# A four-layer image network on one core: the frequency gate cut into links, with the pyramid of means on GpSimd

## The chip, the cores and the metric

The kernel runs on one core of a Trainium2 chip. The core has a matmul engine (TensorE, PE in the profile; its weight loads are PEld), three engines for other arithmetic (VectorE or DVE, ScalarE or ACT, GpSimd or POOL) and a queue engine that issues transfers (SyncE or SP). Every engine works through its own list of instructions in order and waits on semaphores for the others. The metric is the device time of one execution in microseconds (us); less is better.

## The reference

The input is a batch of four images of 192 channels and 64 x 64 pixels in fp32. Four layers follow each other: L0 (channel attention, a deformable convolution with a gather, an MLP), L1 (non-local attention), L2 (attention in overlapping windows, a projection, a frequency gate, a gated MLP) and L3 (a depthwise convolution with generated weights). The change touches the frequency gate of L2 alone:

```python
def _hft(x, w, b):
    a = 3.0 * x
    for s in (2, 4, 8):
        pool = x.reshape(B, C, h // s, s, ww // s, s).mean(axis=(3, 5))
        a = a - jnp.repeat(jnp.repeat(pool, s, axis=2), s, axis=3)
    return jax.nn.sigmoid(_dwconv3(a, w, b)) * x
...
out = _hft(_conv1x1(out, proj_w, proj_b), hft_w, hft_b)
x1 = x + out
```

From three times the projected image the means over blocks of 2 x 2, 4 x 4 and 8 x 8 pixels are subtracted; a 3 x 3 depthwise convolution and a sigmoid make a gate of that, and the gate multiplies the projected image.

## The kernel before

The 192 channels lie on 96 partitions in two halves. An image of 4096 pixels is worked on in `NCH` = 8 chunks of `CN` = 512 pixels, which are 8 rows of 64. The four images go through L2's second part one after the other in `rest`, which runs three generators in a row: `project` (projection and frequency gate), `mlp` and `layer3`. For images 0, 1 and 2 the MLP of layer 0 of the next image (`mlp0`) is interleaved with them: each `yield` of the three gives a credit of 0.5 or 1, and for each full credit one part of `mlp0` is issued. Image 3 has no next image; `rest` calls it `alone`. There five of the nine taps of the convolution go to TensorE (`HFT_PE`), as matmuls with diagonal weights (L1169) that GpSimd builds when the stage starts (L264); for images 0 to 2 all nine taps are VectorE's.

In `project` the order of the instructions on each engine is the order in which the code issues them, moved by a scheduler within what buffers and priorities allow, so that pieces of the gate stand between one another and between pieces of `mlp0`.

`first(i)` makes chunk i. Four matmul calls make the projection in PSUM (`pp`, L1197; the trace shows an fp32 matmul call as two records). ScalarE adds the bias and writes `pr` (L1200), of which there are three buffers. VectorE then builds the pyramid of means in 13 instructions: at each of three levels it adds the even and the odd rows into `pt` (L1208: 512, 128 and 32 elements per partition in the three levels) and the even and the odd columns into `pq` (L1211: 256, 64 and 16). Three multiplications by 1/4, 1/16 and 1/64 follow (L1214: 256, 64 and 16), and four additions of a coarser level into the next finer one (L1219: two of 32, two of 128). ScalarE writes three times `pr` into a strip `hft` of ten rows (L1224), of which `strips` holds three in turn, and VectorE subtracts the upsampled means from it in four instructions (L1230). `share(i)` lets GpSimd copy two edge rows between strip i and strip i-1 (L1151 and L1152); before that `get(i)` has GpSimd clear the side columns (L1140, L1141).

`second(i)` works on a chunk whose strip and whose neighbour's first row are there: nine taps for each half of the channels (the first L1175, the others L1177, into `ha`; the last three taps read the row that L1151 copied), the sigmoid on ScalarE (L1237), the product with `pr` (L1239) and the addition to the image `x` (L1240). It runs one chunk behind:

```python
for i in range(NCH):
    first(i)
    yield 0.5
    if i > 0:
        second(i - 1)
        yield 1.0
ahead()
second(NCH - 1)
```

`ahead()` issues the layer norm of the first chunk of `mlp`.

Of the kernel before, what the change touches and what calls it, by code (L numbers as in the profile page):

```python
# [10 lines left out]
F32 = mybir.dt.float32  # L11
I32 = mybir.dt.int32
AF = mybir.ActivationFunctionType
ALU = mybir.AluOpType
# [4 lines left out]
B, C, H, W = 4, 192, 64, 64  # L19
HW = H * W  # L20
P = 96
NCH = 8
CN = HW // NCH
# [46 lines left out]
def conv_seq_kernel(ctx: ExitStack, tc: tile.TileContext, a, out: bass.AP):  # L70
    nc = tc.nc

    def pool_of(**kw):

        return tc.tile_pool(**({} if kw.get("space") == DRAM else {"reuse_waits": "tile"}), **kw)
# [25 lines left out]
    def halves(name, pool=None):  # L101
        return halves_of(name, a[name].rearrange("(k p) n -> p k n", p=P), pool or wpool)
# [156 lines left out]
    def diagonals(name, w, m, taps, pool):  # L259
        p = w.shape[0]  # L260
        t = pool.tile([p, m, len(taps), p], F32, tag=f"diag_{name}", name=f"diag_{name}")
        for k in range(m):
            for j, tap in enumerate(taps):
                nc.gpsimd.tensor_scalar_mul(t[:, k, j, :], ident[:p, :p], w[:, k, tap : tap + 1])  # L264
        return t
# [3 lines left out]
    with pool_of(name="zero", bufs=1) as zp:  # L269
        zero = zp.tile([128, 4 * C], F32, tag="zero", name="zero")  # L270
        nc.gpsimd.memset(zero, 0.0)
        for i in range(2):
            t = dram.tile([TROWS, 4 * C], F32, tag=f"table{i}", name=f"table{i}")
            first, last = 2 * WP + 2, WP + 1 + NT * 128
# [857 lines left out]
    def strips(held):  # L1132


        tiles = {}

        def get(i):
            if i not in tiles:
                t = tiles[i] = held[:, i % held.shape[1]]
                nc.gpsimd.memset(t[:, :, :, 0:1], 0.0)  # L1140
                nc.gpsimd.memset(t[:, :, :, W + 1 : W + 2], 0.0)  # L1141
                if i == 0:
                    nc.gpsimd.memset(t[:, :, 0, 1 : W + 1], 0.0)
                if i == NCH - 1:
                    nc.gpsimd.memset(t[:, :, 9, 1 : W + 1], 0.0)
            return tiles[i]

        def share(i):

            if i > 0:  # L1150
                nc.gpsimd.tensor_copy(get(i - 1)[:, :, 9, 1 : W + 1], get(i)[:, :, 1, 1 : W + 1])  # L1151
                nc.gpsimd.tensor_copy(get(i)[:, :, 0, 1 : W + 1], get(i - 1)[:, :, 8, 1 : W + 1])  # L1152

        return get, share

    def depthwise(strip, w, k, diag, taps, acc, ps, name):


        parts = strip.shape[0]

        def src(tap):
            return strip[:, k, tap // 3 : tap // 3 + 8, tap % 3 : tap % 3 + W]

        to = acc.rearrange("p (r c) -> p r c", c=W)
        last = None
        if taps:
            p = ps.tile([128, CN], F32, tag="t", name=name)[:parts]
            for j, tap in enumerate(taps):
                nc.tensor.matmul(p, lhsT=diag[:, k, j, :], rhs=src(tap), start=j == 0, stop=j == len(taps) - 1)  # L1169
            last = p.rearrange("p (r c) -> p r c", c=W)  # L1170
        for tap in range(9):
            if tap in taps:
                continue
            if last is None:
                nc.vector.tensor_scalar_mul(to, src(tap), w[:, k, tap : tap + 1])  # L1175
            else:
                nc.vector.scalar_tensor_tensor(to, src(tap), w[:, k, tap : tap + 1], last, ALU.mult, ALU.add)  # L1177
            last = to

    def project(b, x, oi, ps, taps, ahead):  # L1180


        with ExitStack() as s:
            sb = s.enter_context(pool_of(name="l2b", bufs=2))
            s1 = s.enter_context(pool_of(name="l2b1", bufs=1))
            projT = halves("projT", s1)
            hft_diag = diagonals("hft", V["l2_hftw"], 2, taps, s1) if taps else None
            get, share = strips(s1.tile([P, 3, 2, 10, W + 2], F32, tag="hft", name=f"hft_{b}"))
            prs = {}

            def first(i):
                pr = sb.tile([P, 2, CN], F32, tag="pr", name=f"pr_{b}_{i}", bufs=3)
                prs[i] = pr
                for h in range(2):
                    p = ps.tile([128, CN], F32, tag="h", name=f"pp_{b}_{i}_{h}")[:P]
                    for k in range(2):
                        nc.tensor.matmul(  # L1197
                            p, lhsT=projT[:, k, bass.ts(h, P)], rhs=oi[:, k, bass.ts(i, CN)], start=k == 0, stop=k == 1
                        )
                    nc.scalar.activation(pr[:, h, :], p, AF.Identity, bias=V["l2_projb"][:, h])  # L1200

                sums = [pr.rearrange("p k n -> p (k n)").rearrange("p (r c) -> p r c", c=W)]
                for lev in range(3):
                    src = sums[-1]
                    nr, ncol = src.shape[1], src.shape[2]
                    pairs = src.rearrange("p (r e) c -> p e r c", e=2)
                    t = sb.tile([P, nr // 2, ncol], F32, tag=f"pt{lev}", name=f"pt_{b}_{i}_{lev}")
                    nc.vector.tensor_tensor(t, pairs[:, 0], pairs[:, 1], ALU.add)  # L1208
                    pairs = t.rearrange("p r (c e) -> p e r c", e=2)
                    q = sb.tile([P, nr // 2, ncol // 2], F32, tag=f"pq{lev}", name=f"pq_{b}_{i}_{lev}")  # L1210
                    nc.vector.tensor_tensor(q, pairs[:, 0], pairs[:, 1], ALU.add)  # L1211
                    sums.append(q)
                for lev in range(1, 4):
                    nc.vector.tensor_scalar_mul(sums[lev], sums[lev], 0.25**lev)  # L1214
                for lev in (2, 1):
                    fine = sums[lev].rearrange("p (r e) (c f) -> p e r c f", e=2, f=2)
                    coarse = sums[lev + 1]
                    for e in range(2):
                        nc.vector.tensor_tensor(  # L1219
                            fine[:, e], fine[:, e], coarse.unsqueeze(3).to_broadcast(list(coarse.shape) + [2]), ALU.add  # L1220
                        )
                t = get(i)
                for k in range(2):
                    nc.scalar.activation(  # L1224
                        t[:, k, 1:9, 1 : W + 1], pr[:, k, :].rearrange("p (r c) -> p r c", c=W), AF.Copy, scale=3.0
                    )
                    for e in range(2):
                        to = t[:, k, 1 + e : 9 : 2, 1 : W + 1].rearrange("p r (c f) -> p r c f", f=2)
                        mean = sums[1][:, 4 * k : 4 * k + 4, :]
                        nc.vector.tensor_tensor(to, to, mean.unsqueeze(3).to_broadcast([P, 4, 32, 2]), ALU.subtract)  # L1230
                share(i)

            def second(i):
                acc = sb.tile([P, 2, CN], F32, tag="acc", name=f"ha_{b}_{i}")
                for k in range(2):
                    depthwise(get(i), V["l2_hftw"], k, hft_diag, taps, acc[:, k, :], ps, f"ht_{b}_{i}_{k}")
                    nc.scalar.activation(acc[:, k, :], acc[:, k, :], AF.Sigmoid, bias=V["l2_hftb"][:, k])  # L1237
                cols = bass.ts(i, CN)
                nc.vector.tensor_tensor(acc, acc, prs.pop(i), ALU.mult)  # L1239
                nc.vector.tensor_tensor(x[:, :, cols], x[:, :, cols], acc, ALU.add)  # L1240

            for i in range(NCH):
                first(i)
                yield 0.5
                if i > 0:
                    second(i - 1)
                    yield 1.0
            ahead()
            second(NCH - 1)
            yield 1.0  # L1250

    def mlp(b, x, sums, sb, ps, taps, hn):

# [266 lines left out]
    second = begun.enter_context(pool_of(name="l0second", bufs=1))  # L1520
    with ExitStack() as s:
        sb = s.enter_context(pool_of(name="l0first", bufs=1))
# [14 lines left out]
    with ExitStack() as s:  # L1537
        sb, pool = (s.enter_context(pool_of(name=n, bufs=1)) for n in ("norms0", "l0d0"))
# [4 lines left out]
    for b in range(B):  # L1543
        with ExitStack() as s:
            sb = s.enter_context(pool_of(name="l1x", bufs=1))
# [22 lines left out]
        sums = stats.tile([P, 2, NCH], F32, tag="sums", name=f"sums_{b}")  # L1568
# [86 lines left out]
```

## Time and profile before

| what | value |
|---|---|
| median of 3 runs | 7346.84 us (7320.97 to 7362.43) |
| the profiled execution | 7341.43 us, span 7339.6 us, granted TensorE clock 0.924 |
| PE busy | 6582.3 us (90% of the span) |
| DVE busy | 5103.1 us (70%) |
| ACT busy | 3759.7 us (51%) |
| POOL busy | 2130.0 us (29%), of which the issue of gathers at L523 1674.8 us |

The profile is a page on one execution, the trace holds its single instructions, and the views named below are tables made of that trace. A duration is the time of one instruction on its engine, waits for other engines left out. On VectorE a new instruction starts about 0.08 us before the record of the one ahead of it ends, so what an instruction takes of the queue is read from the distance between two starts. "Idle before" and "releaser" tell how long an engine stood still ahead of an instruction and who ended that. The stage of `project` stands at about 1992 to 2160 us for image 0, 3692 to 3862 us for image 1, 5420 to 5589 us for image 2 and 6880 to 6993 us for image 3.

### The profile page before, as it was taken

The numbers are of one execution on the slowest core, as the hardware profiler recorded it, in microseconds if no ns is written. First come the engines' busy times: TensorE is split into PE (matmuls) and PEld (weight loads), VectorE is DVE, ScalarE is ACT, GpSimd is POOL, SyncE is SP. The second block draws the span as 40 slices with busy tenths as digits, with TensorE's granted clock in tenths as the row PEclk, the third lists the DMA queues.
The fourth block names the chain that finished last, engine by engine and source line by source line (L and its number), as shares of the span: only waits on it lengthen the run. The fifth ranks groups of instructions, "written<-read, shape, count | busy, mean of one in ns | idle before, by whom it ended". The sixth has DMA issues, their size and how long they took to land.

```text
span 7339.6 us, 114369 instructions
## 1 busy us (share of the span) xinstructions
PE 6582.3 (90%) x44432; PEld 4260.3 (58%) x44432; DVE 5103.1 (70%) x8016; ACT 3759.7 (51%) x6154; POOL 2130.0 (29%) x2404
## 2 busy tenths in 40 slices
PE   7677999998988799998989889999998889989987
PEld 3444478885534358886634348886653447766543
DVE  3654169984687759994596849995577857755767
ACT  3654258874443258884543338884443325535332
POOL 2653047752200027771200016773210000002100
PEclk8878989998989899998999989998898979989998
DMA  7784146651000166762010066663000010010000
GB/s 231 258 304 143 54 147 219 217 175 34 23 25 14 41 213 212 224 211 56 9 32 18 15 185 207 217 219 116 12 26 21 11 49 9 14 27 19 2 5 19
DMA packets 346940, 740.37 MB, mean 101 GB/s; under 512 B 42151, under 2 KB 224087, under 8 KB 346014
## 3 DMA queue, kind: packets, MB, share of 16 engines
q0 software_dynamic: 95040, 467.22, 19.7%
q1 hardware_dynamic: 251358, 265.85, 12.2%
q8 instruction: 350, 5.73, 0.3%
q14 instruction: 192, 1.57, 0.1%
HBM read 626.44 MB, written 106.21 MB: 100 GB/s over the span
## 4 chain that ended last, share of the span: by engine, by line
PE 67%; DVE 19%; ACT 4%; issue 3%; DMA 3%; POOL 0%; another core or an unknown queue 0%; SPq 0%; ACTq 0%; DVEq 0%; POOLq 0%
PE s L766 11%; PE y L832 11%; PE h L541 7%; DVE ga L1177 5%; DVE ha L1177 3%; PE h L1272 3%; PE v L992 3%; PE h L676 3%; PE o L682 2%; PE qk L917 2%; PE f L1323 2%; PE t L1000 2%; PE qk L918 2%; PE po L433 1%; PE o L1017 1%
## 5 line engine op out<-in xcount | busy, mean ns | idle before, releaser
L523 POOL DMA_INDIRECT ring<-table,idx x1188 | 1674.8, 1410 | 1160.1 <-DVE row L530 270.1
L766 PE MATMUL s<-ths,ph 96*128 96x256 f32 x4096 | 980.3, 386 | 11.0 <-issue 5.8
L766 PEld LDWEIGHTS s<-ths,ph 96*128 96x128 f32 x4096 | 784.0, 193 | 150.0 <-ACT ths L760 14.2
L529 ACT ACTIVATE row<-ring,pos 128x384 f32<-128x384 f32 x1188 | 697.7, 609 | 235.9 <-DVE xo L534 148.6
L530 DVE SCALAR_TENSOR_TENSOR row<-ring,fr,row 128x384 f32<-128x384 f32 x1188 | 699.7, 612 | 100.4 <-ACT row L529 64.6
L832 PE MATMUL y<-sc,gx 128*97 128x256 f32 x3008 | 723.3, 379 | 0.0
L533 ACT ACTIVATE xo<-row,pos 128x192 f32<-128x192 f32 x1188 | 505.6, 449 | 148.3 <-remote 45.0
L832 PEld LDWEIGHTS y<-sc,gx 128*97 128x97 f32 x3008 | 489.4, 164 | 123.1 <-issue 1.1
L1177 DVE SCALAR_TENSOR_TENSOR ga<-gate,v,ga 128x512 f32<-128x512 f32 x720 | 541.4, 752 | 27.6 <-POOL gate L1151 0.2
L534 DVE SCALAR_TENSOR_TENSOR xo<-row,fr,xo 128x192 f32<-128x192 f32 x1188 | 465.3, 411 | 104.5 <-ACT xo L533 51.9
L541 PE MATMUL h<-ti,xo 128*128 128x192 f32 x2376 | 465.0, 330 | 5.6 <-DVE xo L534 5.6
L768 ACT COPY sc<-s 128x1024 f32<-128x1024 f32 x376 | 377.1, 1003 | 175.0 <-PE s L766 160.0
L829 DVE TENSOR_TENSOR sc<-sc,mbs 128x1024 f32<-128x1024 f32 x376 | 448.5, 1217 | 14.8 <-ACT mbs L792 14.3
L773 DVE TENSOR_TENSOR top<-top,sc 128x1024 f32<-128x1024 f32 x282 | 344.3, 1221 | 135.3 <-ACT sc L768 117.8
L541 PEld LDWEIGHTS h<-ti,xo 128*128 128x128 f32 x2376 | 405.7, 191 | 42.8 <-DVE xo L534 10.6
L676 PE MATMUL h<-d_l0m,fc 96*128 96x512 f32 x768 | 362.3, 624 | 66.7 <-DVE d_l0m L333 66.7
L830 ACT ACTIVATE sc<-sc 128x1024 f32<-128x1024 f32 x376 | 393.0, 1054 | 27.8 <-DVE sc L829 18.3
L976 DVE TENSOR_REDUCE es<-ex 128x6 f32<-128x384 f32 x264 | 133.3, 546 | 393.9 <-ACT ex L972 393.9
L541 PE MATMUL h<-kept,xo 128*128 128x192 f32 x990 | 261.4, 401 | 130.0 <-DVE xo L534 68.8
L1272 PE MATMUL h<-d_l2n,fc1T 96*128 96x512 f32 x768 | 351.2, 605 | 23.2 <-DMA fc1T<-scaled_fc1T 15.4
L1151 POOL COPY gate<-gate 128x192 f32<-128x192 f32 x28 | 12.7, 454 | 1190.0 <-ACT gate L1305 1190.0
L682 PE MATMUL o<-gl,fc 128*96 128x512 f32 x768 | 356.1, 614 | 0.0
(318 smaller groups left out, 11563.7 us busy)
## 6 DMA issues: line engine op xcount, KB each, us to landing
ti<-table SPq DMA_DIRECT2D x396, 96.0 KB
table<-tt SPq DMA_DIRECT2D x24, 1056.0 KB
ring<-table,idx POOLq DMA_INDIRECT x1188
xnd<-xn SPq DMA_DIRECT2D x4, 3270.0 KB
table<-kept SPq DMA_DIRECT2D x12, 1056.0 KB
table<-tt SPq DMA_DIRECT2D x44, 288.0 KB
xb<-xnd SPq DMA_DIRECT2D x32, 396.0 KB
xi<-in_x_dram SPq DMA_DIRECT2D x32, 384.0 KB
```

The lines of the kernel that those rows point to most:

```text
L523: nc.gpsimd.indirect_dma_start(out=gt.rearrange("p r q c -> p (r q c)"), out_offset=None, in_=table[:, :], in_offset=bass.IndirectOffsetOn ...
L529: nc.scalar.activation(row, gt[:, :, 0, :], AF.Copy, scale=pos[:, t, 9 + tap : 10 + tap])
L530: nc.vector.scalar_tensor_tensor(row, gt[:, :, 1, :], fr[:, t, 9 + tap : 10 + tap], row, ALU.mult, ALU.add)
L533: nc.scalar.activation(xo[:, j, :], row[:, 0, :], AF.Copy, scale=pos[:, t, tap : tap + 1])
L534: nc.vector.scalar_tensor_tensor(xo[:, j, :], row[:, 1, :], fr[:, t, tap : tap + 1], xo[:, j, :], ALU.mult, ALU.add)
L541: nc.tensor.matmul(acc[m // 2][:, bass.ts(m % 2, C)], lhsT=xo.rearrange("p j c -> p (j c)")[:, bass.ts(m, 128)], rhs=tt, start=t == 0 and ...
L676: nc.tensor.matmul(p, lhsT=fc1[:, k, bass.ts(m, 128)], rhs=hn[:, k, :], start=k == 0, stop=k == 1)
L682: nc.tensor.matmul(p, lhsT=fc2[:, m, bass.ts(h, P)], rhs=gl[:, m, :], start=m == 0, stop=m == 5)
L766: nc.tensor.matmul(p[:, t, :], lhsT=ph[:, bass.ts(G * g + t, 128)], rhs=ths[i], start=True, stop=True)
L832: nc.tensor.matmul(py, lhsT=gx[:, G * g + t, :], rhs=ex[:, t, :], start=g == 0 and t == 0, stop=g == NG - 1 and t == G - 1,)
L1177: nc.vector.scalar_tensor_tensor(to, src(tap), w[:, k, tap : tap + 1], last, ALU.mult, ALU.add)
L1272: nc.tensor.matmul(p, lhsT=fc1b[:, k, bass.ts(m, 128)], rhs=hns[i][:, k, :], start=k == 0, stop=k == 1)
```

## The change

The gate is issued in five links in place of two. `make(i)` holds the projection, the bias and the three times `pr` in the strip. `pyramid(i)` holds the 13 instructions of the pyramid, now on GpSimd. `strip(i)` holds the four subtractions and `share(i)`. `convolve(i)` holds the taps and the sigmoid, and `add(i)` the product with `pr` and the addition to `x`. `make` and `pyramid` run one step ahead of `strip`, and `add` one step behind `convolve`, so `pr` has four buffers in place of three. The credits for `mlp0` are the same.

```diff
@@ -1186,11 +1186,11 @@
             projT = halves("projT", s1)
             hft_diag = diagonals("hft", V["l2_hftw"], 2, taps, s1) if taps else None
             get, share = strips(s1.tile([P, 3, 2, 10, W + 2], F32, tag="hft", name=f"hft_{b}"))
-            prs = {}
-
-            def first(i):
-                pr = sb.tile([P, 2, CN], F32, tag="pr", name=f"pr_{b}_{i}", bufs=3)
-                prs[i] = pr
+            prs, means, accs = {}, {}, {}
+
+            def make(i):
+
+                pr = prs[i] = sb.tile([P, 2, CN], F32, tag="pr", name=f"pr_{b}_{i}", bufs=4)
                 for h in range(2):
                     p = ps.tile([128, CN], F32, tag="h", name=f"pp_{b}_{i}_{h}")[:P]
                     for k in range(2):
@@ -1198,56 +1198,76 @@
                             p, lhsT=projT[:, k, bass.ts(h, P)], rhs=oi[:, k, bass.ts(i, CN)], start=k == 0, stop=k == 1
                         )
                     nc.scalar.activation(pr[:, h, :], p, AF.Identity, bias=V["l2_projb"][:, h])
-
-                sums = [pr.rearrange("p k n -> p (k n)").rearrange("p (r c) -> p r c", c=W)]
+                t = get(i)
+                for k in range(2):
+                    nc.scalar.activation(
+                        t[:, k, 1:9, 1 : W + 1], pr[:, k, :].rearrange("p (r c) -> p r c", c=W), AF.Copy, scale=3.0
+                    )
+
+            def pyramid(i):
+
+                sums = [prs[i].rearrange("p k n -> p (k n)").rearrange("p (r c) -> p r c", c=W)]
                 for lev in range(3):
                     src = sums[-1]
                     nr, ncol = src.shape[1], src.shape[2]
                     pairs = src.rearrange("p (r e) c -> p e r c", e=2)
                     t = sb.tile([P, nr // 2, ncol], F32, tag=f"pt{lev}", name=f"pt_{b}_{i}_{lev}")
-                    nc.vector.tensor_tensor(t, pairs[:, 0], pairs[:, 1], ALU.add)
+                    nc.gpsimd.tensor_tensor(t, pairs[:, 0], pairs[:, 1], ALU.add)
                     pairs = t.rearrange("p r (c e) -> p e r c", e=2)
                     q = sb.tile([P, nr // 2, ncol // 2], F32, tag=f"pq{lev}", name=f"pq_{b}_{i}_{lev}")
-                    nc.vector.tensor_tensor(q, pairs[:, 0], pairs[:, 1], ALU.add)
+                    nc.gpsimd.tensor_tensor(q, pairs[:, 0], pairs[:, 1], ALU.add)
                     sums.append(q)
                 for lev in range(1, 4):
-                    nc.vector.tensor_scalar_mul(sums[lev], sums[lev], 0.25**lev)
+                    nc.gpsimd.tensor_scalar_mul(sums[lev], sums[lev], 0.25**lev)
                 for lev in (2, 1):
                     fine = sums[lev].rearrange("p (r e) (c f) -> p e r c f", e=2, f=2)
                     coarse = sums[lev + 1]
                     for e in range(2):
-                        nc.vector.tensor_tensor(
+                        nc.gpsimd.tensor_tensor(
                             fine[:, e], fine[:, e], coarse.unsqueeze(3).to_broadcast(list(coarse.shape) + [2]), ALU.add
                         )
-                t = get(i)
+                means[i] = sums[1]
+
+            def strip(i):
+
+                mean, t = means.pop(i), get(i)
                 for k in range(2):
-                    nc.scalar.activation(
-                        t[:, k, 1:9, 1 : W + 1], pr[:, k, :].rearrange("p (r c) -> p r c", c=W), AF.Copy, scale=3.0
-                    )
                     for e in range(2):
                         to = t[:, k, 1 + e : 9 : 2, 1 : W + 1].rearrange("p r (c f) -> p r c f", f=2)
-                        mean = sums[1][:, 4 * k : 4 * k + 4, :]
-                        nc.vector.tensor_tensor(to, to, mean.unsqueeze(3).to_broadcast([P, 4, 32, 2]), ALU.subtract)
+                        of = mean[:, 4 * k : 4 * k + 4, :]
+                        nc.vector.tensor_tensor(to, to, of.unsqueeze(3).to_broadcast([P, 4, 32, 2]), ALU.subtract)
                 share(i)
 
-            def second(i):
-                acc = sb.tile([P, 2, CN], F32, tag="acc", name=f"ha_{b}_{i}")
+            def convolve(i):
+                acc = accs[i] = sb.tile([P, 2, CN], F32, tag="acc", name=f"ha_{b}_{i}")
                 for k in range(2):
                     depthwise(get(i), V["l2_hftw"], k, hft_diag, taps, acc[:, k, :], ps, f"ht_{b}_{i}_{k}")
                     nc.scalar.activation(acc[:, k, :], acc[:, k, :], AF.Sigmoid, bias=V["l2_hftb"][:, k])
-                cols = bass.ts(i, CN)
+
+            def add(i):
+                acc, cols = accs.pop(i), bass.ts(i, CN)
                 nc.vector.tensor_tensor(acc, acc, prs.pop(i), ALU.mult)
                 nc.vector.tensor_tensor(x[:, :, cols], x[:, :, cols], acc, ALU.add)
 
+            make(0)
+            pyramid(0)
             for i in range(NCH):
-                first(i)
+                if i + 1 < NCH:
+                    make(i + 1)
+                strip(i)
+                if i + 1 < NCH:
+                    pyramid(i + 1)
                 yield 0.5
+                if i > 1:
+                    add(i - 2)
                 if i > 0:
-                    second(i - 1)
+                    convolve(i - 1)
                     yield 1.0
             ahead()
-            second(NCH - 1)
+            add(NCH - 2)
+            convolve(NCH - 1)
             yield 1.0
+            add(NCH - 1)
 
     def mlp(b, x, sums, sb, ps, taps, hn):
```

## The prediction

> **What bounds the kernel now.** The first view is the page's chain of work that ended last. It says who carries the end of the program.
>
> ```profile
> PE 67%; DVE 19%; ACT 4%; issue 3%; DMA 3%; POOL 0%; another core or an unknown queue 0%; SPq 0%; ACTq 0%; DVEq 0%; POOLq 0%
> ```
>
> The matmul engine carries two thirds, but that is a mean over stages; the change lies in four stages of 113 to 170 us. The second view is busy time by window, one row for each of them.
>
> ```profile
> core 0: us, PE busy (x) PEld busy (x) DVE busy (x) ACT busy (x) POOL busy (x), PEclk, DMA share, GB/s
> 1990.00:2165.00 175.00, 136.64 (x392) 56.19 (x392) 164.95 (x330) 71.22 (x92) 8.90 (x31) 0.86 0.11 31
> 3692.00:3867.00 175.00, 138.16 (x400) 56.62 (x400) 165.80 (x330) 71.61 (x93) 10.23 (x39) 0.87 0.12 33
> 5420.00:5595.00 175.00, 139.70 (x390) 57.66 (x389) 165.88 (x330) 71.66 (x93) 8.87 (x30) 0.86 0.10 29
> 6878.00:6995.00 117.00, 113.25 (x284) 44.19 (x284) 101.92 (x223) 38.08 (x55) 12.48 (x48) 0.96 0.02 6
> ```
>
> For images 0 to 2 VectorE is busy 165 of 175 us and bounds the stage; TensorE has 38 us to spare. For image 3 TensorE bounds it: 113 of 117 us, and 15.00 of 15 us (36 records, 0.42 us each) in the window from 6905. A chunk there has 4 projection and 10 tap calls, 28 records, 11.8 to 12.0 us; the chain's pitch is 12.4 to 12.6. GpSimd has 9 to 12 us to do in each stage.
>
> **What is removed from VectorE.** Instructions there overlap, so I take distances between starts in the timeline, not durations.
>
> ```profile
> 2069.18 0.27 DVE L1208 TENSOR_TENSOR pt<-pq 96x128 f32<-96x128 f32 x1
> 2069.38 0.73 DVE L1177 SCALAR_TENSOR_TENSOR ha<-hft,v,ha 96x512 f32<-96x512 f32 x1
> 2070.04 0.20 DVE L1211 TENSOR_TENSOR pq<-pt 96x64 f32<-96x64 f32 x1
> 2070.18 0.28 DVE L1214 TENSOR_SCALAR pq<-pq 96x256 f32<-96x256 f32 x1
> 2070.38 0.17 DVE L1208 TENSOR_TENSOR pt<-pq 96x32 f32<-96x32 f32 x1
> ```
>
> The second level's row sum takes 0.20 us of the queue, its column sum 0.14, the first multiplication 0.20. The same way the other rows give 0.60 and 0.33 for the first level, 0.10 and 0.09 for the third, 0.10 and 0.08 for the other multiplications, 2 x 0.10 and 2 x 0.20 for the four additions: 2.44 us a chunk, 19.5 us an image. A tap takes 0.66. The waits of VectorE for a sigmoid ahead of L1239 (2.8, 1.0 and 1.0 us in images 0, 1, 2; 1.6 in image 3) go too, since the product stands a step behind: 1.6 us an image.
>
> **What it costs on GpSimd.** No pyramid ran there, so its price is bounded by rows of other lines. L1038 is an addition of two SBUF tiles of 128 elements.
>
> ```profile
> L1038 POOL TENSOR_TENSOR ot<-ot,ot x80: 445/453/1140, 1767.9 to 6877.1; 102x128 f32<-102x128 f32 x40, 96x128 f32<-96x128 f32 x40
> ```
>
> With 0.19 us for a copy of 8 elements (L1450) as the fixed part, that is 2.0 ns an element. The six sums (512, 256, 128, 64, 32, 16) then take 1.22, 0.71, 0.45, 0.32, 0.25 and 0.22 us, together 3.2; the four additions 2 x 0.25 + 2 x 0.45 = 1.4; the multiplications 0.9 by the slope of the copies (0.85 ns an element from 128 to 528) and 1.7 by that of L264 (96 elements 512 ns, 128 elements 601 ns). An undisturbed pyramid: 5.5 to 6.3 us, against 3.3 us on VectorE alone at 1998 us.
>
> It won't be undisturbed, and VectorE neither. The next view is the timeline where both meet.
>
> ```profile
> 1951.99 1.58 POOL L1038 TENSOR_TENSOR ot<-ot,ot 102x128 f32<-102x128 f32 x2 [15.24 <-ACT ot L1032]
> 1952.13 1.13 DVE L967 TENSOR_TENSOR ex<-ex,mx 128x768 f32<-128x768 f32 x1
> ```
>
> L967 takes 0.958 us alone and 1.134 to 1.139 us in each of the 8 cases where L1038 was running as it started: 0.18 us lost, the 0.26 us that 128 elements take less 0.08. GpSimd's second instruction lasted 0.86 to 1.14 us in place of 0.45, until VectorE's was over. So each delays the other. I price VectorE's loss by that row: element time less 0.08 us, which gives 0.95, 0.43, 0.18 and 0.05 us for the four largest sums, 0.36 for the additions, and 0.14 to 0.72 for the multiplications: 2.1 to 2.7 us a pyramid. Instructions with two SBUF inputs, L967's kind, are 120 of 139 us of VectorE's work without the pyramid (L1177 89.7, L1230 11.4, L1239 and L1240 19.3), so 1.8 to 2.3; I take 2.0. That gives back most of the 2.44 saved. The nearest row with taps speaks for less: a 128-element row copy costs a neighbouring tap 0.03 us.
>
> The page "SBUF — State Buffer" of the Trainium skill (§ Who interferes with whom) speaks against the change more strongly: a two-input VectorE instruction and a GpSimd instruction that reads SBUF exclude each other for the whole instruction. With whole GpSimd durations lost (5.9 x 0.86, an estimate) the sum below would be some +60 us in place of +7; the 0.18 us measured behind a 0.45 us instruction speaks for the data part alone.
>
> **Does the pyramid keep up?** GpSimd under pressure waits for the end of a VectorE instruction each time, as the row copies show:
>
> ```profile
> 2055.04 2.13 DVE L1177 SCALAR_TENSOR_TENSOR ha<-hft,v,ha 96x512 f32<-96x512 f32 x3
> 2055.24 0.72 POOL L1152 COPY hft<-hft 96x128 f32<-96x128 f32 x1
> ```
>
> 0.72 us in place of 0.29. Thirteen instructions with some 0.4 us of waiting each on top of 5.9 us: 10 to 12 us a pyramid, and 1.3 us of copies. A step of images 0 to 2 lasts 18.8 us, and `strip(i+1)` needs the pyramid a step later: covered. In image 3 a step is 12 us: just covered, since VectorE, rid of 2.4 us, has gaps there.
>
> **The other moves.** GpSimd's queue gets memsets (`get`, which wait for `convolve(i-2)`), L1151, L1152, then the pyramid; tap 6 of each half waits for L1151 of the next strip, as before, and that copy can now stand behind the rest of a late pyramid. `make` a step ahead moves four matmul calls and four ScalarE passes, and the 3x copy waits for the strip that `convolve(i-2)` has read, a step earlier: nothing, with ScalarE at 41%; no DMA is issued in the loop. With no such cover a pass costs 0.65 us a chunk.
>
> **The sum.** Images 0 to 2: the first pyramid has no cover, about 6.2 for 3.3 us, +3. The second has only the first strip and five taps of `convolve(0)` ahead of it, 4.5 us against 8 to 9: a wait of 4.4 us, less the 2.4 that chunk 1 saves. That is +5 at the start (bounds 0 to +8). The other six chunks: -6 x 2.44 = -14.6, contention +6 x 2.0 = +12, sigmoid waits -1.6. Sum +0.8 an image, +2.4 for three. Image 3: bound by TensorE, so at most 0.5 us a chunk is to be had (12.5 to 12.0, -4); its first tap waits for a pyramid on GpSimd that stands behind ten L264 (5 us) and the memsets, +4 to +5, and the second likewise +4: +4 (0 to +8). In all about +7 us on the 7341.4 us of the profiled execution, 7348. That execution lies 5.4 us below the median, so against the median: 7354 us, or 7337 to 7377 with the terms at their bounds. A measurement of this kernel can tell about 0.5%, 37 us, from no change.
>
> **Rivals.** *The port costs nothing.* The taps and the row copies argue for it (0.03 us each), the 8 cases of L967 against. Without the contention an image gains 5 - 14.6 - 1.6 = -11, three -34, image 3 nothing: 7313; with no loss at the start -21 an image and -4 in image 3: -67, 7280. Chance 0.24, of which 0.18 lie beyond 37 us.
>
> *GpSimd is held out* (slower). Where VectorE runs taps back to back, GpSimd need not get in at every boundary:
>
> ```profile
> 2535.59 5.56 POOL L1450 COPY out<-v 96x8 f32<-96x8 f32 x4 [11.66 <-DMA out_dram<-out]
> 2535.59 5.51 DVE L1456 SCALAR_TENSOR_TENSOR out<-x,w,out 96x504 f32<-96x504 f32 x8
> ```
>
> There a copy of 8 elements, 0.19 us alone, ended only with the eighth L1456. Of 58 such copies 26 met VectorE and 6 waited some 5 us. At 6 in 26 a pyramid has three such waits, 15 us on top of 11: more than the 18.8 us of a step. Then the subtractions L1230 stand and wait with all of VectorE behind them; during that wait GpSimd is free, so I take 4 us a step and not 7: 3 x 7 x 4 = 84, in image 3 7 x 4 = 28, with the +7 about +119, 7466. It decides from a pyramid of some 16 us on. Against it, the row copies of the gate among its taps, none of which took over 0.75 us:
>
> ```profile
> L1152 POOL COPY hft<-hft x28: 288/618/752, 2003.0 to 6959.8; 96x128 f32<-96x128 f32 x28
> ```
>
> Chance 0.33.
>
> *The change gives nothing because VectorE isn't the bound* (another engine or the parts of `mlp0` take its place): 7347. TensorE with 38 us to spare speaks against it. Chance 0.07.
>
> **Numbers.** The even trade has 0.36, of which 0.05 lie beyond 37 us. Faster 0.18; same 0.31 + 0.06 + 0.07 = 0.44; slower 0.33 + 0.05 = 0.38. The range leaves out half of the fast rival's far end and the worse half of the slow one: 7303 to 7430.
>
> **What would show it.** In the changed profile: the stages' lengths (now 168, 169, 169 and 113 us); the durations of GpSimd's sums (0.45 alone and about 1 us with contention for 128 elements); the mean of L1177 in the stage (738 ns now; with 2 us more a chunk on 18 taps some 0.1 us more); VectorE's waits for GpSimd ahead of the subtractions, near none after the second chunk if the pyramid keeps up, 4 us each if it is held out; and in image 3 TensorE's idle ahead of its first taps. The forecast is wrong if taps keep their duration (then faster) or the subtractions wait in every chunk (then slower).

## The result and the profile after

The changed kernel takes 7425.65 us (median of 4 runs, 7405.27 to 7446.65); beside it the kernel before took 7341.31 us. The ratio is 1.0107 with a 95% interval of 1.008 to 1.0135: slower by about 79 us. That is inside the range of the prediction, but it is not the even trade that the prediction held for likeliest. The chain of waits and the busy time of the same four stages, now longer:

```profile
PE 65%; DVE 17%; ACT 4%; issue 3%; DMA 3%; POOL 2%; another core or an unknown queue 0%; SPq 0%; ACTq 0%; DVEq 0%; POOLq 0%
```

```profile
core 0: us, PE busy (x) PEld busy (x) DVE busy (x) ACT busy (x) POOL busy (x), PEclk, DMA share, GB/s
2008.00:2183.00 175.00, 126.86 (x366) 51.40 (x364) 157.00 (x225) 69.91 (x91) 81.31 (x134) 0.84 0.09 26
3732.00:3907.00 175.00, 126.78 (x361) 50.62 (x359) 156.54 (x224) 69.91 (x91) 81.12 (x134) 0.84 0.09 26
5456.00:5631.00 175.00, 126.37 (x361) 50.87 (x359) 156.51 (x224) 69.91 (x91) 81.26 (x134) 0.84 0.09 26
6922.00:7076.00 154.00, 117.74 (x270) 43.78 (x271) 87.45 (x118) 36.77 (x53) 69.81 (x157) 0.86 0.03 7
```

GpSimd has come into the chain with 2%. In images 0 to 2 it is busy 81 us in place of 9, and VectorE, with a hundred instructions less, is busy only 8 to 9 us less. In image 3 neither TensorE nor VectorE is full any more.

To see where the time went I cut each image in the timeline at three points: the end of the last L1067 (the windows are done), the end of the last product with the gate (L1239 before, L1249 after, chunk 7) and the end of the last matmul of fc1 in `mlp` (L1272, now L1292). The stage is from the first to the second, the tail from the second to the third. By these cuts image 0's stage was 171.0 us before, not the 168 of the prediction.

| kernel | stage of image 0, 1, 2, 3 (us) | tail of image 0, 1, 2, 3 (us) | sum |
|---|---|---|---|
| before | 171.0, 169.2, 169.9, 113.1 | 274.0, 273.5, 273.5, 238.7 | 1683 |
| before, once more | 169.3, 171.0, 171.0, 113.1 | 274.0, 274.6, 273.5, 240.1 | 1687 |
| after | 171.8, 172.0, 171.8, 145.3 | 283.8, 283.8, 283.8, 252.4 | 1765 |

The sum grew by 82 us, and the rest of the program by 7 (5657 to 5664 us). So the loss has two places: the stage of image 3, +32 us, and the four tails, +10, +10, +10 and +14. The stages of images 0 to 2, where most of the prediction's working lay, grew by 1 to 3 us.

**Image 3.** VectorE waits for the pyramid ahead of the subtractions of every chunk:

```profile
DVE hft L1238 <- POOL pq L1226: 51.5, 8, 14.9
DVE ha L1249 <- ACT ha L1245: 6.3, 8, 0.8
```

The chain of waits over one chunk says what stands in series (start, length, what; lines between left out):

```profile
6995.03 0.76 DVE ha L1177
6995.81 0.72 ACT ha L1245
6996.53 0.58 ACT pr L1200
...
6997.19 1.74 POOL pt L1215
...
6998.99 1.49 POOL pq L1218
...
7004.07 0.82 POOL pq L1226 x2
7004.91 1.43 DVE hft L1238 x4
7006.34 0.67 DVE ha L1177
```

The last tap, the sigmoid, the bias of `pr`, 7.7 us of pyramid on GpSimd, the subtractions, the first tap of the next chunk. From one L1238 to the next, 6988.34 to 7004.91, it is 16.6 us, in place of 12.4 to 12.6. While the pyramid runs, VectorE has only a product and an addition (L1249, L1250) in its queue, and then stands idle for 4.9 us:

```profile
6993.47 2.31 DVE L1177 SCALAR_TENSOR_TENSOR ha<-hft,v,ha 96x512 f32<-96x512 f32 x3
6996.57 1.22 DVE L1249 TENSOR_TENSOR ha<-ha,pr 96x1024 f32<-96x1024 f32 x1 [0.79 <-ACT ha L1245]
6997.82 2.17 DVE L1250 TENSOR_TENSOR x<-x,ha 96x1024 f32<-96x1024 f32 x1
7004.91 1.43 DVE L1238 TENSOR_TENSOR hft<-hft,pq 96x256 f32<-96x256 f32 x4 [4.92 <-POOL pq L1226]
```

The cause is the order in that queue. In the code, `convolve(2)` is issued in step 3 and `strip(4)` in step 4, so the taps of chunk 2 would cover pyramid 4. In the queue as the trace shows it for image 3 the subtractions of strips 0, 1 and 2 come first, then taps 0, strip 3, taps 1, strip 4, taps 2: the scheduler has moved each strip ahead of the taps that should cover its pyramid. On ScalarE the sigmoids of chunk 1 stand ahead of the bias of chunk 4. So pyramid 4 begins when taps 1 are done, and taps 2 when pyramid 4 is. In images 0 to 2 the queue has taps 1 ahead of strip 3, as in the code.

**The tails.** The chain of waits at the end of image 0's gate:

```profile
2179.12 0.73 ACT ha L1245
...
2179.88 1.23 DVE ha L1249
...
2181.12 0.02 SPq L107
...
2181.17 4.50 DMA fc1T<-scaled_fc1T
...
2185.81 8.77 PE h L1292 x12
```

The weights `fc1T` of the MLP are loaded into room that the gate's tiles leave. Before, that room (6 KB from the bottom of the pool) had held `pr` of chunks 5 and 6, and the load went out after the product of chunk 6, at 2150.4 us, 13 us ahead of the last product. With four buffers of `pr` the room holds chunk 7 as its second buffer, and the load waits for the last product, L1249. TensorE, which before had begun fc1 beside the last taps, stands still until the weights land. Its wait for them is 62.6 us over the four images; before it was 15.4 in three of them. The load and the wait, first of the kernel before, then the wait after:

```profile
L107 SPq DMA_DIRECT2D fc1T<-scaled_fc1T x4: 327/328/331, 2150.4 to 6980.6; - x4
  DMA fc1T<-scaled_fc1T: 15.4, 3
```

```profile
  DMA fc1T<-scaled_fc1T: 62.6, 4
```

### The profile page after: what moved, and what is told of

It reads as the page before. It is cut to its first block, busy times and chain, and to the rows that moved or that the text cites. A ratio compares the mean times of both kernels' runs of the same rounds, so it can differ in the third digit from the quotient of the medians.

```text
span 7428.4 us, 114286 instructions
## 1 busy us (share of the span) xinstructions
PE 6590.0 (89%) x44432; PEld 4259.3 (57%) x44432; DVE 5065.5 (68%) x7600; ACT 3759.5 (51%) x6151; POOL 2398.6 (32%) x2820
## 3 DMA queue, kind: packets, MB, share of 16 engines
q1 hardware_dynamic: 251358, 265.85, 12.1%
## 4 chain that ended last, share of the span: by engine, by line
PE 65%; DVE 17%; ACT 4%; issue 3%; DMA 3%; POOL 2%; another core or an unknown queue 0%; SPq 0%; ACTq 0%; DVEq 0%; POOLq 0%
PE s L766 11%; PE y L832 10%; PE h L541 6%; DVE ga L1177 5%; PE h L1292 3%; DVE ha L1177 3%; PE v L992 3%; PE o L682 2%; PE h L676 2%; PE qk L917 2%; PE f L1343 2%; PE t L1000 2%; PE qk L918 2%; PE o L1017 1%; PE pm_l2n L311 1%
## 5 line engine op out<-in xcount | busy, mean ns | idle before, releaser
L1177 DVE SCALAR_TENSOR_TENSOR ga<-gate,v,ga 128x512 f32<-128x512 f32 x720 | 541.4, 752 | 27.6 <-POOL gate L1151 0.2
L1151 POOL COPY gate<-gate 128x192 f32<-128x192 f32 x28 | 12.4, 442 | 1263.5 <-ACT gate L1325 1263.5
L1292 PE MATMUL h<-d_l2n,fc1T 96*128 96x512 f32 x768 | 356.4, 613 | 70.4 <-DMA fc1T<-scaled_fc1T 62.6
```

The lines of the kernel that those rows point to most:

```text
L1292: nc.tensor.matmul(p, lhsT=fc1b[:, k, bass.ts(m, 128)], rhs=hns[i][:, k, :], start=k == 0, stop=k == 1)
```

## The experiments

Theory A: image 3's loop and the room of the weights carry the loss. Theory B, the rival: GpSimd and VectorE delay each other at SBUF, in all images, and the loss follows the engine. The first four kernels ran beside a kernel before of 7347 us; kernels 5 to 8 on a second chip, where it takes 7270 us, and kernels 9 to 11 on a third, where it takes 7260. Ratios are to the kernel before of the same set; the stages come from each kernel's trace.

| kernel | ratio (95%) | stages (us) | tails (us) | sum |
|---|---|---|---|---|
| 1 order only | 1.0038 (1.0011 to 1.0065) | 170.9, 169.1, 169.2, 110.8 | 282.6, 283.1, 282.5, 252.8 | 1721 |
| 2 weights | 1.0085 (1.0054 to 1.0116) | 174.8, 174.5, 178.3, 145.2 | 274.1, 274.6, 274.6, 246.1 | 1742 |
| 3 image 3 on VectorE | 1.0093 (1.0061 to 1.0125) | 171.8, 174.3, 174.1, 112.4 | 284.0, 282.8, 283.3, 255.0 | 1738 |
| 4 code order | 1.0094 (1.0061 to 1.0127) | 178.1, 178.0, 174.2, 124.8 | 283.9, 284.0, 283.2, 252.7 | 1759 |
| 5 no pyramid | 0.9944 (0.9919 to 0.9969) | 148.3, 149.5, 148.1, 104.6 | 283.7, 284.5, 283.7, 252.5 | 1655 |
| 6 mix | 0.9961 (0.9939 to 0.9982) | 166.1, 167.9, 165.1, 112.9 | 274.0, 274.5, 274.6, 244.3 | 1679 |
| 7 two more sums | one run, 7356.5 us | 188.1, 190.1, 187.9, 145.2 | 282.6, 284.0, 282.7, 252.7 | 1813 |
| 8 old order, GpSimd | 1.0070 (1.0038 to 1.0101) | 189.4, 191.6, 190.2, 142.1 | 274.4, 274.4, 275.0, 238.7 | 1776 |
| 9 weights, all on VectorE | 1.0016 (1.0001 to 1.0031) | 171.6, 169.2, 169.3, 111.1 | 273.1, 275.0, 273.5, 246.1 | 1689 |
| 10 mix again | 0.9988 (0.9962 to 1.0014) | 165.1, 167.4, 166.7, 111.0 | 274.3, 274.0, 274.6, 246.1 | 1679 |

**1. The order alone.**

```diff
 def pyramid(i):
-    nc.gpsimd.tensor_tensor(...)   # and the other twelve
+    nc.vector.tensor_tensor(...)
```

> The five links and their order kept, the 13 instructions of the pyramid back on VectorE. Theory A (order and room): the loss of some 85 us is +32 in image 3, where VectorE's queue puts strip(i+2) ahead of the taps of chunk i so that the pyramid on GpSimd stands in series with the taps, and +10 to +14 in each of the four images because the weights fc1T wait for the last product with the gate, L1249 of chunk 7. The first goes here, the second stays: 7375 to 7390 us. Theory B (port): the loss is GpSimd and VectorE delaying each other; with GpSimd out of it the time is that of before, 7335 to 7350.

7373.8 us, and in the trace +38 us to the kernel before: +41 in the tails, -3 in the stages. The five links with the pyramid on VectorE keep the late weights (PE's wait for `fc1T` is 66.0 us) and lose the loop of image 3. The median lies 1 us under the range of theory A and well over that of theory B.

**2. The room of the weights.**

```diff
+low = s.enter_context(pool_of(name="l2p", bufs=2))
 sb = s.enter_context(pool_of(name="l2b", bufs=2))
...
-t = sb.tile([P, nr // 2, ncol], F32, ...)
+t = low.tile([P, nr // 2, ncol], F32, ...)     # and q
```

> The changed kernel with the pyramid's tiles pt and pq in a pool of their own below pr, so that fc1T takes their room and waits for the subtractions of chunk 7 in place of the product of chunk 7. Theory A: PE's wait for fc1T (62.6 us over four images) goes, 35 to 45 us less: 7380 to 7392 us, perhaps 10 lower since fc1T now comes earlier than in the kernel before, too. Theory B: nothing, 7420 to 7430.

The tails fall by 9.7, 9.2, 9.2 and 6.3 us, to those of before but for 7 us in image 3. What TensorE waits for ahead of fc1 no longer has the load in it:

```profile
L107 SPq DMA_DIRECT2D fc1T<-scaled_fc1T x4: 332/400/401, 2153.8 to 7030.9; - x4
...
  DVE d_l2n L333: 7.5, 10
```

In the first image it went out at 2153.8 us, 23 us ahead of the first fc1 matmul (2177.1). That fc1, counted from the last product, begins only 2 to 3 us earlier than before in images 0 to 2, and no earlier in image 3, fits this last line: once the weights are there, it waits for the layer norm (`d_l2n`). The whole kernel gained less than expected (7400 us), since its stages of images 0 to 2 were 2.5 to 6.5 us longer than in the changed kernel; kernel 4, whose code for images 0 to 2 is that of the changed kernel, shows the same 174 to 178 us, so that this is how a stage with GpSimd in it scatters.

**3. Image 3 on VectorE.**

```diff
+on = nc.vector if taps else nc.gpsimd     # taps: image 3 only
-nc.gpsimd.tensor_tensor(...)
+on.tensor_tensor(...)
```

> The changed kernel with the pyramid of image 3 alone on VectorE. Theory A: the serial loop of image 3 goes, its stage is some 113 us to the last product in place of 145: 30 to 36 us less, 7390 to 7397 us. Theory B: a quarter of the loss, about 20 us less, 7405.

7398.6 us, a little over theory A's range and under theory B's figure; image 3's stage is 112.4 us in place of 145.3. This says that the 32 us need GpSimd, not yet whether its queue or the contention makes them.

**4. Code order.**

```diff
+with ExitStack() as order:
+    if taps:
+        order.enter_context(tc.manual_schedule())
     make(0)
     ...
```

> The changed kernel with the instructions of image 3's gate held in the order of the code, so that the taps of chunk i-1 stand ahead of strip(i+1) on VectorE; the pyramid stays on GpSimd. Theory A: the pyramid of 8 to 11 us is covered by the taps, the pitch of a chunk falls from 16.6 to 12 to 13 us: 22 to 30 us less, 7395 to 7403 us. Theory B: the pyramid on GpSimd is as slow as before or slower with taps beside it, 7425.

With the pyramid still on GpSimd image 3's stage falls to 124.8 us, and the products of chunks 0 to 7 end 89.8 us apart, as before (90.0), in place of 105.1. TensorE is full again, and GpSimd beside it:

```profile
6930.00:6990.00 60.00, 59.65 (x132) 22.45 (x133) 47.12 (x67) 15.54 (x25) 51.05 (x88) 0.95 0.00 0
```

So 15 of the 32 us are the pitch, and the order made it. Another 5 came back at the start, and the 12 that remain are there: the first product ends 35.0 us after the windows in place of 23.1 (40.2 in the changed kernel), behind two pyramids of GpSimd that nothing covers. GpSimd isn't the whole of that: with the pyramid on VectorE in the same links the first product ends 29 to 31 us after the windows (kernels 1, 3, 9 and 10), so that 6 to 8 of the 12 belong to the links. Theory B expected no gain.

The mean over seven distances hides that the loop itself became faster than before. From the second product to the sixth they start 12.0 us apart, where the kernel before had 12.4 to 12.6. Then one distance is 16.8 us: in the order of the code the layer norm of `ahead()` stands ahead of the product of chunk 6, and VectorE waits in it.

```profile
6995.95 1.31 DVE L1249 TENSOR_TENSOR ha<-ha,pr 96x1024 f32<-96x1024 f32 x1
7007.98 1.30 DVE L1249 TENSOR_TENSOR ha<-ha,pr 96x1024 f32<-96x1024 f32 x1
7020.56 0.95 DVE L325 RECIPROCAL r_l2n<-r_l2n 128x128 f32<-128x128 f32 x1 [2.80 <-ACT r_l2n L323]
7023.62 1.28 DVE L333 TENSOR_TENSOR d_l2n<-d_l2n,pb_l2n 96x512 f32<-96x512 f32 x2 [2.11 <-PE pb_l2n L299]
7024.82 1.21 DVE L1249 TENSOR_TENSOR ha<-ha,pr 96x1024 f32<-96x1024 f32 x1
```

The single pyramid in the loop is longer here (8.6 to 10.0 us beside taps, 7.7 in the changed kernel), and costs the loop nothing: without any pyramid (kernel 5) the distance is 12.0 us too.

**5 and 7. No pyramid, and two more sums.**

```diff
 # 5
+still = s1.tile([P, 8, W // 2], F32, tag="still", name=f"still_{b}")
+nc.gpsimd.memset(still, 0.0)
 def pyramid(i):
+    means[i] = still
 # 7, in images 0 to 2
+for e in range(2):
+    spare = sb.tile([P, 8, W], F32, tag=f"spare{e}", name=f"spare_{b}_{i}_{e}")
+    nc.gpsimd.tensor_tensor(spare, flat[:, 0], flat[:, 1], ALU.add)
```

> The changed kernel with the pyramid left out on every engine: the subtractions take a tile of zeros. It shows the stage of images 0 to 2 without GpSimd's sums. Theory A: from the end of the windows to the last product 171.8 us now; the taps and their neighbours regain the 12.3 us by which their distances between starts grew in image 0, and the two waits of 13.4 us for the pyramid go: 148 to 155 us in images 0 to 2, and about 108 us in image 3, where the matmuls set 12 us a chunk. In all some 40 us less from image 3, 60 from the others. Theory B: the same for images 0 to 2.

> The changed kernel with two more sums of 512 elements per chunk on GpSimd in images 0 to 2, whose result nobody reads: the suspected contention raised by a known amount. By the rule of the prediction (element time less 0.08 us, on 87% of the time) a sum costs VectorE 0.83 us, +13 us an image; by what the trace of the changed kernel shows (1.5 us a pyramid where that rule gave 2.0) +10 us; if the delay on VectorE were no cost but only a wait, 0. GpSimd's pyramid grows to some 15 us, under the 18.8 us of a step, so the subtractions should not wait more than now after the second chunk.

Image 0's stage by window: first of the kernel before, then of the changed kernel, without the pyramid, and with two more sums. VectorE has the same 223 instructions in the last three:

```profile
1993.30:2164.30 171.00, 133.83 (x376) 53.95 (x374) 162.61 (x326) 71.22 (x92) 8.89 (x30) 0.86 0.10 27
```

```profile
2009.50:2181.30 171.80, 125.36 (x358) 50.51 (x356) 154.82 (x223) 69.91 (x91) 81.31 (x134) 0.84 0.09 24
```

```profile
1932.40:2080.70 148.30, 118.40 (x358) 49.06 (x356) 142.83 (x223) 74.52 (x95) 12.03 (x30) 0.90 0.10 28
```

```profile
1917.90:2106.00 188.10, 130.32 (x359) 51.67 (x357) 168.63 (x223) 69.67 (x91) 106.90 (x150) 0.81 0.08 22
```

The same instructions of VectorE are busy 142.8, 154.8 and 168.6 us. Eight pyramids on GpSimd cost it 12.0 us, 1.5 each; sixteen more sums of 512 elements cost 13.8 us, 0.86 each. The contention is there, at the size that L967 and L1038 gave before the change (0.83 for such a sum). The stage of kernel 5, 148 to 150 us as expected, is what the pyramid's move could have given at the most in this order. Kernel 7's stages grew by 16 to 18 us, more than the 10 or 13 expected: the 13.8 of contention, and waits for the pyramid that grew by 2.0 us in image 0.

**6 and 10. The mix.**

```diff
+on = nc.vector if taps or i < 2 else nc.gpsimd     # with the pool of kernel 2
```

> The changed kernel with three of the causes taken out: the pyramid's tiles lie below pr, so that the weights fc1T don't wait for the last product; image 3's pyramid is VectorE's; and in images 0 to 2 the first two pyramids are VectorE's, where it has nothing else to do, the other six GpSimd's. Theory A: 10 us an image from the weights, 31 in image 3, 6 to 10 at the start of images 0 to 2: about 90 us less than the changed kernel, 7325 to 7342 us, level with the kernel before or up to 0.2% faster. Theory B: the contention of images 0 to 2 stays, about 7390.

> The combination (pyramid's tiles below pr, image 3 and the first two pyramids on VectorE) once more: it came out 0.39% faster than before, of which the stages of the trace showed only 4 us (0.05%). If the stages are right, 0.995 to 1.002; if something outside them became faster, 0.996 again.

The start of images 0 to 2 gives 4 to 7 us, the tails are those of before, and the sum is 1679 us both times, 4 to 7 us (0.05 to 0.1% of the program) under that of the kernel before. The first set gave 0.9961, 0.4% under the kernel before; the second 0.9988 with 1 inside its interval. The stages account for some 5 us of it; the rest of the first set's gain is not explained. It beats the changed kernel in any case.

**8. The engine alone.**

```diff
 # kernel before, in first(i)
-nc.vector.tensor_tensor(t, pairs[:, 0], pairs[:, 1], ALU.add)    # and the other twelve
+nc.gpsimd.tensor_tensor(t, pairs[:, 0], pairs[:, 1], ALU.add)
```

> The kernel before with its pyramid on GpSimd, in the old two links: the engine alone, without the order. Theory A: the pyramid of a chunk stands ahead of its subtractions in the same step, VectorE has only the taps that its queue puts ahead of them; in image 3 the loop is as in the changed kernel, and the weights wait as in the kernel before: +30 in image 3, and up to 8 us of waiting a chunk in images 0 to 2 where few taps stand ahead: 7390 to 7480. Theory B: contention is the same as in the changed kernel, 7425.

+18 to +22 us a stage in images 0 to 2, +29 in image 3, the tails as before: 1.0070. Waits for the pyramid carry it, in image 0:

```profile
DVE hft L1230 <- POOL pq L1219: 30.5, 6, 10.5
```

Issuing the pyramid a step ahead does its work in images 0 to 2: it cuts that wait to 13.4 us. Of what the links win there, 56 us in three stages, 45 are given back in the tails and image 3: the sums are 1776 and 1765 us, and the intervals of the two ratios overlap.

**9 and 11. VectorE with the weights in time, and the kernel before again.** Kernel 9 is kernel 1 with the pool of kernel 2; kernel 11 has no edit.

> The five links and their order, the whole pyramid on VectorE in all images, and the pyramid's tiles below pr. Theory A, from the stages of the first two sets of runs: 171, 169, 169 and 111 us to the last product and 274, 274, 274 and 245 us from there to the last matmul of fc1, in all 1687 us, 4 more than before: level with the kernel before, within 0.2%, and 8 us more than with GpSimd's share of six pyramids an image. If GpSimd is worth nothing or a loss, it is level with that kernel or below it.

> The kernel before, unaltered, for a trace on the same chip: how far the stages of one kernel scatter. Expected within 2 us of 171, 169, 170 and 113 us to the last product and 274, 274, 274 and 239 us after it, and another 5650 us for the rest of the program if the chip is like the first.

Kernel 9 has a sum of 1689 us: the links are worth nothing measurable by themselves, and GpSimd's six pyramids some 3 us an image. The kernel before gave the same stages within 2 us, 1687 in all, while the part of the program ahead of image 0's gate took 1934 us on this chip and 1993 in the first profile. That is why the stages tell more here than the whole times do.

## Why the prediction was right or wrong

**The stages of images 0 to 2: right.** Forecast +0.8 us each, measured +0.8, +2.8 and +1.9. That near is in part luck: the same instructions gave stages of up to 178 us in kernel 4. The terms, in image 0:

| term | forecast (us) | measured (us) |
|---|---|---|
| undisturbed pyramid on GpSimd | 6.2 | 6.4 (2012.79 to 2019.19 us) |
| contention | +12 for six pyramids | +12.0 for eight (kernel 5) |
| contention of a 512-element sum | 0.83 | 0.86 (kernel 7) |
| VectorE's waits for the pyramid | two at the start, +3 and +4.4 | 9.9 (with the wait for the first `pr`, 4.9 before) and 3.4, no other |

The size of the contention was off by a quarter, 1.5 us a pyramid in place of 2.0; the two sums agree since the forecast charged six pyramids and the trace eight. The removal of 19.5 us (19.8 between kernels before and 5) less 12.0 of contention is 7.8 us less work, and VectorE's idle time grew by 8.6 (8.4 to 17.0 us): together the +0.8. VectorE's wait for the sigmoid went from 2.8 to 0.8 us. The mean of L1177 rose by 0.06 us, not the 0.1 forecast, since the subtractions and the products bore part of the contention:

```profile
L1177 DVE SCALAR_TENSOR_TENSOR ha<-hft,v,ha 96x512 f32<-96x512 f32 x128 | 94.8, 793 | 0.6 <-POOL hft L1151 0.6
L1238 DVE TENSOR_TENSOR hft<-hft,pq 96x256 f32<-96x256 f32 x32 | 14.4, 504 | 13.4 <-POOL pq L1226 13.4
```

**Image 3: wrong, in the step "Does the pyramid keep up?".** Forecast +4 (0 to +8), measured +32. The step took a pyramid of a chunk to have a whole step of cover, as the code issues it and as the queue has it in images 0 to 2. In image 3's queue it has none, and a chunk takes 16.6 us. "Just covered" was right for the order of the code: kernel 4, in that order and with the pyramid on GpSimd, has the forecast 12.0 us, as has kernel 5 without a pyramid; kernels 9 and 10, with VectorE's, have 12.1. The start was mis-sized as well: +17 us in the changed kernel and +12 in kernel 4, in place of +8.

**The tails: missing.** "The other moves" counted what the moved steps issue, and buffers only as the reason for a fourth `pr`. It did not ask who gets that room next. The product of chunk 7 is the gate's last in both kernels; before, its `pr` lay outside the weights' room, and the fourth buffer put it under them. That is +44 us in the trace of the changed kernel, of which kernel 2 takes back 34. Some 4 to 7 us of image 3's tail stay in kernels 2, 6, 9 and 10. There TensorE waits 1.9 us for a gelu ahead of `zm` (kernel 9), and the granted clock is lower just behind the gate. Two windows of kernel 9, from 2 us behind the last product, and the same two of the kernel before:

```profile
6900.00:6910.00 10.00, 8.61 (x16) 3.77 (x17) 2.53 (x2) 5.60 (x8) 0.00 (x0) 0.83 0.00 0
6910.00:6920.00 10.00, 7.70 (x64) 5.12 (x63) 4.80 (x5) 3.89 (x7) 0.00 (x0) 0.83 0.00 0
```

```profile
6997.00:7007.00 10.00, 7.69 (x56) 3.62 (x55) 2.95 (x3) 6.29 (x8) 2.21 (x4) 1.00 0.00 1
7007.00:7017.00 10.00, 10.00 (x35) 5.30 (x36) 4.58 (x5) 5.35 (x7) 0.00 (x0) 1.00 0.00 0
```

Kernels 2 and 10 have the same 0.83 there. Why the clock was lower stays open.

**The range.** That 7425.65 us lies inside 7303 to 7430 is luck. The slow end of the range stood for GpSimd held out, which the trace shows in 6 instructions of 416; the two costs that brought the time there, a serial loop of +32 us in place of +4 and late weights at +44 in place of nothing, weren't in the sum.

**The rivals.** *The port costs nothing* fell: 12 us an image. *GpSimd is held out* had the right sign, with +119 us for about +79, and the wrong reason. Of the 416 instructions of the pyramids in the trace of the changed kernel, 6 took over 1 us longer than their shortest (2.5 to 3.5 us longer), all of them first sums, two an image in images 0 to 2; one is the 4.71 us here (minimum, median and maximum in ns, image 0):

```profile
L1215 POOL TENSOR_TENSOR pt<-pr x8: 1259/1692/4713, 2012.8 to 2118.7; 96x512 f32<-96x512 f32 x8
```

Three such waits a pyramid were forecast for that case. The subtractions did wait in every chunk of image 3, but for a pyramid of 7.7 us, hardly disturbed, that began late. Theory B is left with 12 us an image, which VectorE's saving pays for.

**The page's rule.** By the page "SBUF — State Buffer" of the Trainium skill (§ Who interferes with whom) the one that comes second is blocked until the other's instruction is over. That this loses whole GpSimd durations, some +60 us by the prediction's estimate, did not come: a pyramid of 6.4 us cost VectorE 1.5. A sum of 1.26 us on GpSimd cost it 0.86 on average, and no tap of the gate in the changed kernel took over 1.76 us, 1.02 more than its usual 0.74. How far into GpSimd's instruction VectorE came each time isn't known, so these numbers neither show nor exclude a block to its end.

## What to carry to other kernels

When work goes to another engine "a step ahead", read the step from the queue of the engine that waits, in each variant of the loop: a scheduler may move the consumer ahead of the cover, and then the moved work stands in series. When a pool gets one buffer more, look up who takes that room next, and behind whose last use; here a load of 4.5 us, hidden for the most part before, cost 10 us an image. And cut the trace at a few fixed points: the stages of the kernel before agree within 2 us where the whole program scatters by 40.

## What the runs showed of the hardware

Against a queue of VectorE instructions with two SBUF inputs, GpSimd's sum of 512 elements took 2.19 us on average in image 0 (1.26 alone), and each cost VectorE 0.86 us: between the two engines 13 instructions with 2.44 us of VectorE's queue became 1.5 us of delay there, so that 0.9 us a chunk was all that the move could win on VectorE.

```profile
L1215 POOL TENSOR_TENSOR pt<-pr 96x512 f32<-96x512 f32 x8 | 17.5, 2185 | 14.4 <-ACT pr L1200 14.4
L1221 POOL TENSOR_SCALAR pq<-pq 96x256 f32<-96x256 f32 x8 | 8.5, 1057 | 0.0
```

The multiplication of 256 elements by a constant takes 0.85 us undisturbed, more than a sum of two tiles of as many elements (0.61); by the prediction's two slopes it lies between 0.41 and 0.96. And a stage in which GpSimd stands beside VectorE scatters more than one without: 171.8 to 178.3 us in images 0 to 2 over the changed kernel and kernels 2 to 4, 169.1 to 171.6 over the kernel before, twice, and kernels 1 and 9.
